# Attention row sums: one tile moved from TensorE's sums to VectorE, four sum matmuls placed behind the values, residual bias by accumulating DMAs

## The chip, the cores and the metric

The kernel runs on one core of one Trainium2 chip. A core has five engines with a queue each: TensorE (PE), VectorE (DVE), ScalarE (ACT), GpSimd (POOL) and SyncE (SP); each works through its own queue in order and waits on semaphores for the others. SP issues most DMAs; POOL issues the accumulating and the indirect ones. [...]

The metric is the device time of one execution in microseconds (us), lower is better, as the median over the runs. The profile is one more execution, taken by the hardware profiler; its own device time and its span (first to last instruction) are given beside the median below.

## The reference

A transformer block on 2 sequences of 1,024 tokens, 512 wide, in float32: attention with 16 heads of 32 and low-rank updates on all four projections, a residual and a layer norm; then a mixture of 8 experts with a capacity of 256 tokens each, a shared expert, a residual and a layer norm. Cut to what matters here:

```python
def lora_linear(x, W, b, Bm, Am):
    out = jnp.einsum('bld,od->blo', x, W) + b
    upd = jnp.einsum('blr,or->blo', jnp.einsum('bld,rd->blr', x, Bm), Am)
    return out + SCALING * upd
...
scores = jnp.einsum('bhqd,bhkd->bhqk', q, k) * SCALE
attn = jax.nn.softmax(scores, axis=-1)
out = jnp.einsum('bhqk,bhkd->bhqd', attn, v)
B, H, L, hd = out.shape
out = out.transpose(0, 2, 1, 3).reshape(B, L, H * hd)
return lora_linear(out, Wo, bo, Bo, Ao)
...
x = _layernorm(x + _L0_attn_ref(x, ...), axis=-1)
x = _layernorm(x + _L0_ffn_ref(x, ...), axis=-1)
```

## The kernel before

**Stages.** Projections of q, k and v come first (to about 157 us of the span), then the attention loop (to about 600), with the output projection of the first sequence inside it and that of the second at its end, then the router, the shared expert and the experts. The change touches the attention loop and what is fed into it.

**Units and steps.** A unit is four heads of one sequence against half of its queries (512): 16 units (`NU`). A unit has eight steps, one for each 128 keys: 128 steps `t = 8u + k` (`NS`). A step has four quarters, one per head. In a quarter PE computes the scores of 128 keys by 512 queries into PSUM (`st`, L638), and ACT takes the exponential of them into a tile `pt` in SBUF (L647); two heads share a `pt` tile of 128x1024, so a step makes two, "pair 0" and "pair 1", from a pool of 13 buffers (`PTB`). The `st` banks come from a pool of three.

**The order is written out by hand.** In this loop the instructions of all engines stand in program order (`manual_schedule`). For each quarter the loop collects a list `between[q]`, and `st_step` runs the list after that quarter's score and exponential. Into these lists go, at places given by tables at the top of the file:

- `maxima` (`S_AT`): one score tile `s` of 128 queries by 512 keys on PE (L203) and its row maximum on DVE (L211), for a unit one and a half ahead. There are 32 a unit; `s` has four PSUM banks. After a unit's last one the maxima are gathered (L214), transposed on PE (L221), split into a high and a low part (`mh` on ACT, L224; `ml` on DVE, L225), and two DMAs on SP write them as two rows into that unit's query tile (L227). The next unit's scores read these rows, so that the maximum is subtracted within the score matmul.
- `av_step` (in the fourth quarter of even steps, `AVQ`): the values, PE matmuls of 128x32 by 128x512 for the two steps before (L657), accumulated in PSUM over a unit; `av_out` copies them out on ACT in step 0 of the next unit (L671).
- `adds` (`ADDS`): the row sums of the exponentials, tile by tile. In a unit up to the 14th: step 1's tile is the base `accs`; tile 2 is added to it and tile 3 to tile 0 by accumulating DMAs that POOL issues (L682); tiles 4, 5, 6 and 0 are added on POOL (L685), for both pairs. Units 14 and 15 add on DVE instead.
- `finish` (`FIN`): the sum over partitions. Matmuls with a ones matrix (L698) turn `accs` into sums in PSUM, four matmuls, one per head; tiles named by `DIRECT` get four matmuls of their own. Then ACT copies the sums (`rc`, L712), SP writes them to DRAM (`sd`, L714) and reads them back spread over partitions (`r`, L716).
- `invert` (`REC`): the reciprocal on DVE (L722), written to DRAM (L723) and read back as rows for all partitions (`rb`, four DMAs, L726), all on SP.
- `normalize` (`NRM`): in the unit after next of its own, in three parts: DVE multiplies the values by `rb` (L738), ACT rounds the product to its high part (L743), DVE forms the low part (L745).
- `oproj` (`OPROJ_AT`): the output projection of the first sequence (L771), in units 8 to 10; DVE adds the residual row (L776) and starts the norm.
- `load_res` (`RES_AT`) reads a tile of 128 rows of the residual on SP (L750); `add_res` (`RES_ADDS`) adds the bias of the output projection to it on POOL (L754). There are 16 such tiles.

At a unit's first step SP also loads the keys (in even units, two ahead) and queries (L166, L186) of units to come. A matmul of these float32 kinds (`av`, `sm`) shows as two entries in the profile.

Which tables the change rewrites: `DIRECT`, `FIN`, `REC`, `NRM`, `S_AT`, `OPROJ_AT`, `RES_ADDS`; which lines of the loop: the place of `finish_max(NU - 1)` and of `add_res`, and a new function beside `adds`. The entry of a table under `None` holds for all units that have no entry of their own; a triple is (units later, step, quarter). A step of `S_AT` has four pairs: maxima ahead of and behind the values and the sum of that quarter.

Of the kernel before, what the change touches and what calls it, by code (L numbers as in the profile page):

```python
# [13 lines left out]
ALU = mybir.AluOpType  # L14
# [5 lines left out]
B, L, D = 2, 1024, 512  # L20
NU = 16
# [11 lines left out]
LEAD = 12  # L33
LATE, OP_ONE = (0,), 0
NS = NU * 8
# [15 lines left out]
MAN3 = {mybir.EngineType.PE}  # L51
MAN4 = MAN2 - MAN3

DIRECT = {None: (7,), NU - 2: (), NU - 1: (6, 7)}
AVQ = 3


FIN = {None: (1, 4, 1), NU - 3: (1, 3, 1), NU - 2: (1, 2, 3)}
REC = {None: (1, 6, 3), NU - 3: (1, 5, 1)}
NRM = {  # L60
    None: ((2, 3, 0), (2, 3, 0), (2, 3, 2)),
    NU - 3: ((1, 7, 3), (1, 7, 3), (1, 7, 3)),
    NU - 2: ((1, 4, 1), (1, 4, 1), (1, 4, 1)),
}


S_AT = (
    ((2, 0), (0, 0), (1, 0), (0, 0)), ((0, 0), (2, 0), (1, 0), (0, 1)),
    ((0, 0), (1, 1), (0, 1), (0, 0)), ((0, 0), (1, 1), (0, 1), (0, 1)),
    ((0, 1), (1, 1), (1, 1), (2, 0)), ((0, 0), (0, 2), (1, 0), (0, 1)),  # L70
    ((0, 1), (1, 0), (1, 0), (0, 0)), ((0, 1), (0, 1), (0, 1), (0, 1)),
)
XTB = 2


# [2 lines left out]
    NU - 2: {1: "bb1 dd01", 3: "dd23 vv4", 4: "vv5", 5: "vv6", 6: "vv3 vv7"},  # L78
    NU - 1: {1: "bb1 dd01", 3: "dd23 vv4", 4: "vv5", 6: "vv3"},
}  # L80
OPROJ_AT = (68, 70, 72, 74, 76, 78, 80, 82)
RES_AT = tuple(8 * i + (2 if i % 2 else 6) for i in range(8)) + (70, 74, 86, 90, 100, 102, 106, 110)
RES_ADDS = tuple(t + 3 for t in RES_AT[:14]) + (114, 115)
RB = 2
BTB = 4
AHEAD = 5
# [26 lines left out]
def kernel(  # L113
# [3 lines left out]
    pe, act, dve, pool, sp = nc.tensor, nc.scalar, nc.vector, nc.gpsimd, nc.sync  # L117

    def f(ap):
        return ap.bitcast(F32)  # L120
# [16 lines left out]
    bo_bc = const.tile([P, D], F32, name="bo_bc")  # L137
# [25 lines left out]
    def load_k(g, cs=slice(0, 1024), hs=slice(0, 4)):  # L163
        kt = Ks[g % 2]
        for blk, hl in ((0, 0), (1, 1), (2, 0)):
            sp.dma_start(  # L166
                out=f(kt[32 * blk : 32 * blk + 32, hs, cs]),
                in_=qk_d[1, g // NG, g % NG, hl].rearrange("(h p) t -> p h t", p=32)[:, hs, cs],
            )

    def load_v(g):
        if g < NG:
            vts[g] = x1b[:, :, g * P : g * P + P]
        else:
            vts[g] = mp_.tile([P, 8, P], F32, name=f"vt{g}", tag="vt", bufs=2)
        sp.dma_start(
            out=vts[g],
            in_=v_d[g // NG].rearrange("(c p) d -> p c d", p=P)[
                :, :, (g % NG) * P : (g % NG) * P + P
            ],  # L180
        )

    def load_q(u, hs=slice(0, 4)):
        g, qb = u // 2, u % 2
        for blk, hl in ((0, 0), (1, 0), (2, 1)):
            sp.dma_start(  # L186
                out=f(Qs[u % 3][32 * blk : 32 * blk + 32, hs]),
                in_=qk_d[0, g // NG, g % NG, hl].rearrange("(h p) t -> p h t", p=32)[
                    :, hs, qb * 512 : qb * 512 + 512
                ],  # L190
            )

    mts, pts, avs, accs, vts = {}, {}, {}, {}, {}
# [25 lines left out]
    def finish_max(u):  # L219
        mp = one.tile([P, 512], F32, name=f"mp{u}", tag="one")  # L220
        pe.transpose(mp[0:16, 0:P], mts[u], ident)  # L221
        mh = mp_.tile([16, P], F32R, name=f"mh{u}", tag="mh", bufs=2)
        ml = mp_.tile([16, P], F32R, name=f"ml{u}", tag="ml", bufs=2)
        act.copy(mh, mp[0:16, 0:P])  # L224
        dve.tensor_tensor(ml, mp[0:16, 0:P], f(mh), ALU.subtract)  # L225
        for i, m_ in enumerate((mh, ml)):
            sp.dma_start(  # L227
                out=f(Qs[u % 3][96 + i : 97 + i, :, :]).rearrange(
                    "o h (q t) -> o (h q) t", t=P
                ),  # L230
                in_=f(m_),
            )
# [236 lines left out]
    def new_xt(nm, i):  # L469
        if i % 2 == 0:  # L470
            pairs[nm] = [
                po["flx"].tile([P, KC, 512], F32R, name=f"xt{q}{nm}{i}", tag=f"xt{q}", bufs=XTB)
                for q in "hl"
# [120 lines left out]
    x1 = (x1a, x1b)  # L594
# [24 lines left out]
    with ph2, tc.manual_schedule(engines={mybir.EngineType.PE}):  # L619
# [31 lines left out]
        def av_step(t):  # L651
            u, kc = t // 8, t % 8
            g = u // 2
            if kc == 0:
                avs[u] = avp.tile([P, 512], F32, name=f"av{u}", tag="av")
            for h in range(4):
                pe.matmul(  # L657
                    avs[u][32 * h : 32 * h + 32, :],
                    vts[g][:, kc, 32 * h : 32 * h + 32],
                    pts[t, h // 2][:, h % 2, :],  # L660
                    start=kc == 0,
                    stop=kc == 7,
                    skip_group_check=True,
                )
# [4 lines left out]
        def av_out(u):  # L669
            raws[u] = ap.tile([P, 512], F32, name=f"ae{u}", tag="ae", bufs=2)  # L670
            act.copy(raws[u], avs[u])  # L671

        def adds(t):
            u, kc = t // 8, t % 8
            for op in ADDS.get(u, ADDS[None]).get(kc, "").split():
                i = u * 8 + int(op[2])
                for pr in range(2):
# [5 lines left out]
                    else:  # L683
                        eng = dve if op[pr] == "v" else pool
                        eng.tensor_tensor(accs[u, pr], accs[u, pr], pts[i, pr], ALU.add)  # L685

        def direct(u):
            return DIRECT.get(u, DIRECT[None])

# [57 lines left out]
        def load_res(n):  # L747
            b, i = divmod(n, 8)
            r0 = b * L + i * P
            sp.dma_start(out=x1[b][:, i, 0:D], in_=x[r0 : r0 + P, :])  # L750

        def add_res(n):
            b, i = divmod(n, 8)
            pool.tensor_tensor(x1[b][:, i, 0:D], x1[b][:, i, 0:D], bo_bc, ALU.add)  # L754

        later = []
        rows1 = {}
# [26 lines left out]
        def run(gen):  # L784
            for _ in gen:
                pass
# [12 lines left out]
        def at_step(table, t, q):  # L799
            for v in range(max(t // 8 - 2, 0), t // 8):  # L800
                at = table.get(v, table[None])
                at = at[q] if isinstance(at[0], tuple) else at
                if (v + at[0]) * 8 + at[1] == t:
                    yield v

        for t in range(NS):
            u, k = t // 8, t % 8
            if k == 0:

                if u % 2 == 0 and 2 <= u and u // 2 + 1 < B * NG:  # L810
                    for hs in (slice(0, 2), slice(2, 4)):
                        load_k(u // 2 + 1, hs=hs)
                        load_q(u + 2, hs)
                elif u >= 1 and u + 2 < NU:
                    load_q(u + 2)
                if u % 2 and NG <= u // 2 + 1 < B * NG:
                    load_v(u // 2 + 1)
            if t in RES_AT:
                load_res(RES_AT.index(t))
            between = [[], [], [], []]  # L820
            for q in range(4):
                between[q] += [maxima] * S_AT[k][q][0]
            if t + LEAD == NS + 1:
                between[0].append(lambda: finish_max(NU - 1))

            if t and t % 2 == 0:
                between[AVQ].append(lambda: (av_step(t - 2), av_step(t - 1)))
                if k == 0:
                    between[AVQ].append(lambda: av_out(u - 1))
            for v in at_step(FIN, t, 0):  # L830
                between[FIN.get(v, FIN[None])[2]].append(lambda v=v: finish(v))
            for q in range(4):
                between[q] += [maxima] * S_AT[k][q][1]
            if t:
                between[AVQ].append(lambda: adds(t - 1))
            for q in range(3):
                for v in at_step(NRM, t, q):
                    between[NRM.get(v, NRM[None])[q][2]].append(lambda v=v, q=q: normalize(v, (q,)))
            for v in at_step(REC, t, 0):
                if v < RDIR:  # L840
                    between[REC.get(v, REC[None])[2]].append(lambda v=v: invert(v))
            if t in RES_ADDS:
                between[3].append(lambda: add_res(RES_ADDS.index(t)))

            if t in OPROJ_AT:
                op0 = oproj(0, OPROJ_AT.index(t), OPER)
                for q in range(3):
                    between[q].append(lambda q=q, op0=op0: run(op0) if q == 2 else next(op0))
            st_step(t, between)
            for _, fn in [x for x in later if x[0] == 0]:  # L850
                fn()
            later[:] = [(n - 1, fn) for n, fn in later if n]
            if t - NS >= OPROJ1:
                next(op10, None)
# [349 lines left out]
    for st, (blk, nb) in enumerate(BLOCKS):  # L1204
        hss = []
        for c in range(6):
# [9 lines left out]
            if c == 0 and blk + nb == NB:  # L1216
                reads_xd(
                    sp.dma_start(
                        out=meta, in_=xd_d[:, D : D + 2].rearrange("(j p) c -> p j c", p=P)
# [9 lines left out]
            for v in range(c * nb, c * nb + nb):  # L1229
                bv, cv = blk + v // 6, v % 6  # L1230
                n = (bv - NB + 1) * 6 + cv
# [10 lines left out]
    with tc.manual_schedule(engines=MAN4):  # L1242
        last = None
        for e in range(E):
            nxt = e + 1
            hss = []
            for c in range(6):
# [4 lines left out]
                n = nxt * 6 + c  # L1252
# [113 lines left out]
```

## Time and profile before

| | us |
|---|---|
| median of 3 runs | 1041.44 |
| lowest and highest | 1038.62, 1042.34 |
| the profiled execution | 1041.44 |
| its span | 1039.7 |
| mean granted TensorE clock | 0.992 |

Units in the profile, from the first exponential of one to that of the next: 24.25 (unit 0), 25.46, 25.84, 26.93, 25.87, 27.13, 25.86, 26.35 (7), 31.44, 37.64, 32.10 (8 to 10, with the output projection), 27.02, 25.86, 31.76, 24.04 (14).

How to read what follows. A line of a group or of a timeline names the source line, the engine, the operation and the tiles, output before input (buffer numbers left out). In a timeline the first two columns are the start and the length in us; several like instructions in a row are merged (x8), and brackets tell how long the engine was idle before and what released it. In the list of groups the columns after the bar are the busy time in us, the mean length of one in ns, and the idle time just before them. PE's matmuls overlap, so the length of one is more than the distance to the next.

### The profile page before, as it was taken

The numbers are of one execution on the slowest core, as the hardware profiler recorded it, in microseconds if no ns is written. First come the engines' busy times: TensorE is split into PE (matmuls) and PEld (weight loads), VectorE is DVE, ScalarE is ACT, GpSimd is POOL, SyncE is SP. The second block draws the span as 40 slices with busy tenths as digits, with TensorE's granted clock in tenths as the row PEclk, the third lists the DMA queues.
The fourth block names the chain that finished last, engine by engine and source line by source line (L and its number), as shares of the span: only waits on it lengthen the run. The fifth ranks groups of instructions, "written<-read, shape, count | busy, mean of one in ns | idle before, by whom it ended". The sixth has DMA issues, their size and how long they took to land. (4 is left out here: it accounts for less than half of the span.)

```text
span 1039.7 us, 15687 instructions
## 1 busy us (share of the span) xinstructions
PE 1007.0 (97%) x5606; PEld 728.0 (70%) x5606; DVE 684.1 (66%) x1156; ACT 527.8 (51%) x1000; POOL 535.0 (51%) x404
## 2 busy tenths in 40 slices
PE   8999999999999999999989999999999999999994
PEld 6888885555545555655544489888787899999994
DVE  6743788788888887788878773232253467777752
ACT  5322216666767665576657835122122366555662
POOL 5000005989898977869887164000015055666774
PEclk9999999999999999999989999999999999999998
DMA  9866875586868784667964631000009567777621
GB/s 277 289 230 214 245 222 114 126 190 138 190 134 194 154 193 95 127 138 151 197 153 85 151 112 62 22 21 11 31 30 302 177 205 233 258 244 254 222 82 61
DMA packets 87374, 164.75 MB, mean 158 GB/s; under 512 B 15944, under 2 KB 24648, under 8 KB 87296
## 3 DMA queue, kind: packets, MB, share of 16 engines
q1 hardware_dynamic: 74240, 117.59, 38.9%
q0 software_dynamic: 13056, 46.16, 19.9%
q8 instruction: 44, 0.72, 0.3%
q14 instruction: 34, 0.28, 0.1%
HBM read 96.10 MB, written 33.80 MB: 125 GB/s over the span
## 5 line engine op out<-in xcount | busy, mean ns | idle before, releaser
L211 DVE TENSOR_REDUCE mt<-s 128x1 f32<-128x512 f32 x512 | 317.8, 680 | 69.1 <-PE s L203 68.8
L647 ACT ACTIVATE pt<-st 128x512 f32<-128x512 f32 x512 | 266.6, 611 | 113.7 <-PE st L638 107.1
L685 POOL TENSOR_TENSOR pt<-pt,pt 128x1024 f32<-128x1024 f32 x112 | 264.3, 2389 | 37.1 <-ACT pt L647 18.6
L638 PE MATMUL st<-qs,ks 98*128 98x512 f32 x512 | 197.7, 417 | 11.1 <-ACT pt L647 8.8
L203 PE MATMUL s<-ks,qs 96*128 96x512 f32 x512 | 186.8, 403 | 0.2
L638 PEld LDWEIGHTS st<-qs,ks 98*128 98x128 f32 x512 | 92.8, 189 | 94.5 <-ACT pt L647 37.9
L682 POOL DMA_DIRECT2D pt<-pt x64 | 56.2, 1004 | 185.6 <-issue 144.6
L931 PE MATMUL h<-xthe,w13s 128*128 128x256 f32 x704 | 130.0, 283 | 0.0
L203 PEld LDWEIGHTS s<-ks,qs 96*128 96x128 f32 x512 | 97.3, 190 | 36.2 <-DVE mt L211 10.8
L931 PEld LDWEIGHTS h<-xthe,w13s 128*128 128x128 f32 x704 | 110.7, 191 | 0.4
L919 POOL TENSOR_TENSOR w2s<-w2r,w2s 128x512 fp32r<-128x512 f32 x42 | 65.9, 1590 | 68.2 <-ACT w2s L918 65.3
L931 PE MATMUL h<-xtle,w13s 128*128 128x256 f32 x352 | 100.3, 285 | 0.4 <-DVE xtle L484 0.4
L1121 POOL DMA_INDIRECT xd_d<-x1a,slot_i x8 | 7.9, 984 | 139.3 <-DVE slot_i L1118 137.2
L931 PEld LDWEIGHTS h<-xtle,w13s 128*128 128x128 f32 x352 | 67.4, 191 | 1.5 <-DVE xtle L484 0.8
L657 PE MATMUL av<-pt,vt 128*32 128x512 f32 x512 | 62.3, 598 | 0.0
L657 PE MATMUL av<-pt,x1b 128*32 128x512 f32 x512 | 61.6, 598 | 0.0
L1017 PE MATMUL y<-w2s,hs 128*128 128x512 f32 x260 | 60.9, 390 | 0.0
L1017 PEld LDWEIGHTS y<-w2s,hs 128*128 128x128 f32 x260 | 48.2, 188 | 10.2 <-DVE hs L999 0.5
L342 ACT ACTIVATE oh<-o,bqk_sb 128x512 fp32r<-128x512 f32 x32 | 22.0, 690 | 56.2 <-PE o L327 52.5
L586 DVE TENSOR_TENSOR w13s<-x1a,w13s 128x1024 fp32r<-128x1024 f32 x32 | 46.7, 1460 | 4.6 <-issue 4.1
L327 PE MATMUL o<-xh,wh 128*128 128x512 f32 x116 | 45.5, 392 | 1.0 <-DVE ol L343 1.0
L327 PE MATMUL o<-xl,wh 128*128 128x512 f32 x116 | 45.3, 391 | 0.0
(571 smaller groups left out, 1704.2 us busy)
## 6 DMA issues: line engine op xcount, KB each, us to landing
pt<-pt POOLq DMA_DIRECT2D x64, 512.0 KB
x1a<-in_w_dram SPq DMA_DIRECT2D x32, 512.0 KB
w2r<-in_w_dram SPq DMA_DIRECT2D x42, 256.0 KB
ks<-qkd SPq DMA_DIRECT2D x36, 256.0 KB
qkd<-oh SPq DMA_DIRECT2D x32, 256.0 KB
qkd<-ol SPq DMA_DIRECT2D x32, 256.0 KB
qs<-qkd SPq DMA_DIRECT2D x30, 256.0 KB
qs<-qkd SPq DMA_DIRECT2D x36, 128.0 KB
```

What stands on the lines that cost most here:

```text
L203: pe.matmul(s1, Qs[u % 3][0:96, h, qt * P : qt * P + P], Ks[g % 2][0:96, h, kh * 512 : kh * 512 + 512], start=True, stop=True,)
L211: dve.tensor_reduce(mts[u][:, c, kh : kh + 1], s1, AX.X, ALU.max)
L327: pe.matmul(o, lhs, rhs, start=k + i == 0, stop=k + i == KC + 1)
L586: (pool if e < 0 else dve).tensor_tensor(lo, raw, f(hi), ALU.subtract)
L638: pe.matmul(sb, Ks[g % 2][:, h, kc * P : kc * P + P], Qs[u % 3][:, h, :], start=True, stop=True,)
L647: act.activation(pts[t, h // 2][:, h % 2, :], sb, AF.Exp, scale=SCALE)
L657: pe.matmul(avs[u][32 * h : 32 * h + 32, :], vts[g][:, kc, 32 * h : 32 * h + 32], pts[t, h // 2][:, h % 2, :], start=kc == 0, stop=kc == 7 ...
L682: pool.dma_start(out=pts[to, pr], in_=pts[i, pr], accum_op=ALU.add)
L685: eng.tensor_tensor(accs[u, pr], accs[u, pr], pts[i, pr], ALU.add)
L919: pool.tensor_tensor(hl[:, 1, :], raw, f(hl[:, 0, :]), ALU.subtract)
L931: pe.matmul(hp[:, j * 256 : j * 256 + 256], lhs, rhs[:, k, :], start=n == 0, stop=n == 11,)
L1017: pe.matmul(o, lhs, rhs, start=n == 0, stop=n == 16)
```

## The change

The last `pt` tile of a unit (step 7) was summed by PE alone (`DIRECT`, four extra matmuls a unit). It is now added to `accs` by DVE: `add_last`, in the next unit, pair 0 in step 3 behind the third head, pair 1 in step 4 behind the first head, for units 0 to 13. The sum is four matmuls, in the fourth quarter of step 4, behind that quarter's values; it stood in the second quarter. The reciprocal moves from step 6 to step 7, the three parts of the normalization by a few quarters, the maxima are spread anew over the steps, the output projection comes two steps later, the transposing of the last unit's maxima one step earlier. The bias is added to a residual tile by an accumulating DMA that POOL issues, in step 3 of each unit up to the 14th, with four in steps of their own. Units 14 and 15 keep their sums; unit 13's is no longer a case of its own.

```diff
-DIRECT = {None: (7,), NU - 2: (), NU - 1: (6, 7)}
+DIRECT = {None: (), NU - 1: (6, 7)}
 AVQ = 3
...
-FIN = {None: (1, 4, 1), NU - 3: (1, 3, 1), NU - 2: (1, 2, 3)}
-REC = {None: (1, 6, 3), NU - 3: (1, 5, 1)}
+FIN = {None: (1, 4, 3), NU - 2: (1, 2, 3)}
+REC = {None: (1, 7, 1)}
 NRM = {
-    None: ((2, 3, 0), (2, 3, 0), (2, 3, 2)),
-    NU - 3: ((1, 7, 3), (1, 7, 3), (1, 7, 3)),
+    None: ((2, 2, 3), (2, 3, 2), (2, 4, 1)),
+    NU - 3: ((2, 1, 2), (2, 1, 2), (2, 1, 2)),
     NU - 2: ((1, 4, 1), (1, 4, 1), (1, 4, 1)),
 }
...
 S_AT = (
-    ((2, 0), (0, 0), (1, 0), (0, 0)), ((0, 0), (2, 0), (1, 0), (0, 1)),
-    ((0, 0), (1, 1), (0, 1), (0, 0)), ((0, 0), (1, 1), (0, 1), (0, 1)),
-    ((0, 1), (1, 1), (1, 1), (2, 0)), ((0, 0), (0, 2), (1, 0), (0, 1)),
-    ((0, 1), (1, 0), (1, 0), (0, 0)), ((0, 1), (0, 1), (0, 1), (0, 1)),
+    ((0, 1), (0, 0), (0, 1), (1, 1)), ((1, 0), (1, 1), (1, 0), (0, 1)),
+    ((0, 0), (1, 0), (1, 0), (0, 0)), ((1, 0), (0, 1), (0, 0), (2, 0)),
+    ((0, 0), (0, 1), (0, 1), (0, 2)), ((0, 1), (0, 0), (0, 1), (2, 0)),
+    ((0, 1), (0, 1), (0, 0), (1, 1)), ((0, 0), (3, 0), (1, 0), (1, 0)),
 )
+
+
+LAST_AT = ((3, 2), (4, 0))
...
-OPROJ_AT = (68, 70, 72, 74, 76, 78, 80, 82)
+OPROJ_AT = (70, 72, 74, 76, 78, 80, 82, 84)
...
-RES_ADDS = tuple(t + 3 for t in RES_AT[:14]) + (114, 115)
+RES_ADDS = tuple(range(11, 108, 8)) + (107, 114, 115)
...
+        def add_last(u, pr):
+            dve.tensor_tensor(accs[u, pr], accs[u, pr], pts[u * 8 + 7, pr], ALU.add)
+
...
-            pool.tensor_tensor(x1[b][:, i, 0:D], x1[b][:, i, 0:D], bo_bc, ALU.add)
+            pool.dma_start(out=x1[b][:, i, 0:D], in_=bo_bc, accum_op=ALU.add)
...
-            if t + LEAD == NS + 1:
-                between[0].append(lambda: finish_max(NU - 1))
...
+            if t + LEAD == NS:
+                between[AVQ].append(lambda: finish_max(NU - 1))
...
-            if t in RES_ADDS:
-                between[3].append(lambda: add_res(RES_ADDS.index(t)))
+            for pr in range(2):
+                if 0 < u < NU - 1 and LAST_AT[pr][0] == k:
+                    between[LAST_AT[pr][1]].append(lambda pr=pr: add_last(u - 1, pr))
+            for n, at in enumerate(RES_ADDS):
+                if at == t:
+                    between[3].append(lambda n=n: add_res(n))
```

## The prediction

> **What bounds the kernel now.** I read the engine shares first, then the busy time of two neighbouring units of the attention loop, the groups of that loop, and the timelines of units 5 and 6.
>
> ```profile
> PE 1007.0 (97%) x5606; PEld 728.0 (70%) x5606; DVE 684.1 (66%) x1156; ACT 527.8 (51%) x1000; POOL 535.0 (51%) x404
> ```
>
> The windows hold one odd and one even unit:
>
> ```profile
> 285.00:311.00 26.00, 24.60 (x142) 12.65 (x141) 22.25 (x36) 17.23 (x35) 23.84 (x15) 1.00 0.64 134
> 311.00:337.00 26.00, 25.88 (x147) 13.69 (x146) 21.67 (x38) 18.27 (x38) 22.82 (x13) 1.00 0.88 189
> ```
>
> Columns after the length: PE, PEld, DVE, ACT, POOL. PE is full in the even unit; DVE (22) and POOL (23) have about 3 us to spare. Step 0 of units 5, 6 and 7 starts on ACT at 285.22, 312.35 and 338.21: the units take 27.13 and 25.86 us. The groups that the change touches:
>
> ```profile
> L698 PE MATMUL sm<-pt,ones 128*32 128x512 f32 x256 | 33.1, 626 | 0.0
> L738 DVE TENSOR_TENSOR ae<-ae,rb 128x512 f32<-128x512 f32 x14 | 22.7, 1620 | 0.5 <-DMA rb<-rd 0.4
> L685 DVE TENSOR_TENSOR pt<-pt,pt 128x1024 f32<-128x1024 f32 x16 | 18.5, 1209 | 1.7 <-DMA pt<-pt 1.7
> L754 POOL TENSOR_TENSOR x1a<-x1a,bo_bc 128x512 f32<-128x512 f32 x8 | 9.6, 1194 | 0.0
> ```
>
> L738 takes 1.62 us on average, but 0.69 where POOL is not adding. The timeline shows why odd units are longer:
>
> ```profile
> 292.15 2.38 POOL L685 TENSOR_TENSOR pt<-pt,pt 128x1024 f32<-128x1024 f32 x1
> 293.50 2.83 DVE L738 TENSOR_TENSOR ae<-ae,rb 128x512 f32<-128x512 f32 x1
> ...
> 294.48 1.30 POOL L754 TENSOR_TENSOR x1a<-x1a,bo_bc 128x512 f32<-128x512 f32 x1
> ...
> 296.36 0.62 ACT L743 CAST at_h<-ae 128x512 fp32r<-128x512 f32 x1 [1.17 <-DVE ae L738]
> ...
> 297.53 0.50 PE L638 MATMUL st<-qs,ks 98*128 98x512 f32 x1 [1.40 <-ACT pt L647]
> ```
>
> L738 reads two SBUF tiles and ends 0.55 after POOL's second addition (295.78): it was held through both. ACT waits for it, and PE for ACT. Unit 13 does this with two L754 (L738: 4.33 us), and PE's idle time brings the clock down:
>
> ```profile
> 532.99 0.80 PE L638 MATMUL st<-qs,ks 98*128 98x512 f32 x1 [2.63 <-ACT pt L647]
> ...
> 535.00 3.62 PE L698 MATMUL sm<-pt,ones 128*32 128x512 f32 x16
> ```
>
> Sixteen entries take 3.62 us there, not 1.92; the granted clock is 0.5 from 531.64 for 6.83 us.
>
> A second path is nearly as long as PE's. SP's queue in unit 6:
>
> ```profile
> 327.13 0.54 SPq L714 DMA_DIRECT2D sd<-rc  x1
> 332.91 0.33 SPq L716 DMA_DIRECT2D r<-sd  x1
> 333.33 0.52 SPq L227 DMA_DIRECT2D qs<-mh  x1
> 333.94 0.54 SPq L227 DMA_DIRECT2D qs<-ml  x1
> ```
>
> ```profile
> 337.72 0.40 PE L638 MATMUL st<-qs,ks 98*128 98x512 f32 x1
> ```
>
> L716 waits 5.6 us for the sums to land in DRAM, and the maxima's rows (L227), which unit 7's first score reads at 337.72, stand behind it in the queue. By the semaphore updates they land at 336.94, 0.78 us ahead. Over the units without output projection the time from L714 to that landing is 8.3 to 10.4 us, and the margin 0.2 to 2.3.
>
> **The change part by part.** Positions are us from a unit's first score matmul; rows are unit 5's and 6's.
>
> *Sums.* 14 units lose four of eight matmuls (8 of 16 entries). The block takes 1.85 us (324.53 to 326.38) plus 0.2 for switching in and out (0.32 and 0.34 between starts, against 0.234). Eight entries behind the values take 0.85 and switch nothing: 1.2 us less PE time, 14 x 1.2 = 16.7. PE's floor for a plain unit: 64 matmuls x 0.234 + 4 value blocks x 2.05 + 0.85 + transposing 0.27 = 24.3; the same sum gives 25.5 for before (measured 25.86).
>
> *Bias.* 16 POOL additions (19.7 us) become 16 accumulating DMAs. Issuing one took POOL 0.88 us (56.2/64), 14 us in all, in the pause after its last addition. Their data (4 MB) follow the unit's own DMAs on the queue; the first reader is a projection three steps or more later, against a 4 to 7 us landing for twice the size. I cost it at nothing; without that cover it is late by at most one landing, 5 us, once. Without L754, L738 (now a quarter step earlier) waits for one addition at most. Gone are PE waits of 0.60, 1.40, 0.59, 1.25 and 2.63 (at 244, 297, 349, 477, 532), 6.5 us, and half of the 5.5 us at half clock, 2.7: together 9.2.
>
> *DVE.* 28 additions at 1.21 (start to start 1.14, the L685 rows) are 2.3 us a unit, against 0.9 less for L738: DVE goes from 22 to 23.5 of at least 24.3, so it is no bound. Behind them in its queue stand reductions; PE may be four PSUM tiles (2.4 us) ahead before it waits. What the additions wait for, POOL's last one, is done by 9.3 (below); what waits for them is ACT, which now takes the buffers they free at 12.5 and 16.9, and they end at 12.4 and 14.7. ACT's buffers of steps 6 and 7 now wait for the last two accumulating DMAs, which land 9.2 to 14.6 after the first issue (295.72 to 304.92; 215.97 to 230.49), so at 19 to 24.6, and are wanted at 19.7 and 22.5: nothing in odd units, up to 2 in even ones, inside PE's wait at the unit's end (next part); without that wait 2 x 6 = 12.
>
> *Return path.* The sums now end after step 4's values, at 15.5 instead of 14.5; rc and L714 follow 0.75 later, at 16.3. SP's order (L714, L716, L227) is unchanged. Adding 9.4 (the middle of 8.3 to 10.4) and 0.14 (unit 15: 573.78 to 573.92), the next unit's first score can't start before 25.8. PE would be done at 24.3 and waits 1.5. L722 stands at 25 and its operand lands some 0.4 before the maxima's rows (336.57, 336.94), so it may hold DVE 0.5; L738's rows land some 6 after it, 2 ahead of need. So in ten plain units (1 to 7, 11 to 13) the 1.2 us are not gained: 12 of 16.7 are lost. At 8.3 the unit takes 24.7, at 10.4 it takes 26.8: 10 us either way over ten units. Units 8 and 9 had 6.8 us of margin; these, 10 and 14 keep their gain.
>
> *Shared read path.* L738, the additions and L745 (now behind the second one) need POOL not to add. With 0.61 per reduction DVE reaches L738 at 8.7, the additions at 11.3 and 13.6, L745 at 15.5. With units of 25.8 POOL's last addition ends at 7.9 to 9.3 and the next chain starts when the first accumulating DMA lands: its issue waits for step 2's values (9.9 in unit 6, 10.0 now), plus 4.6 in odd units, 6.1 in even ones:
>
> ```profile
> 295.72 1.74 POOL L682 DMA_DIRECT2D pt<-pt  x2
> ...
> 300.33 2.39 POOL L685 TENSOR_TENSOR pt<-pt,pt 128x1024 f32<-128x1024 f32 x1 [0.72 <-DMA pt<-pt]
> 302.92 2.38 POOL L685 TENSOR_TENSOR pt<-pt,pt 128x1024 f32<-128x1024 f32 x1 [0.20 <-DMA pt<-pt]
> ```
>
> So POOL starts at 14.7 (odd) and 16.1 (even). The additions come in time; L745 does by 0.6 in even units, and in the six odd ones (3 to 13) it is 0.8 late. If it gets in at the 0.2 us gap after POOL's first addition it waits 1.6 and PE some 1.5, of which 1.0 lies in the wait at the unit's end: 0.6 x 6 = 3.6. The other end is a rival below; the low end is nothing.
>
> [...]
>
> The order and places of the other steps (maxima, projections two steps later, unit 13's late sum) I take as nothing: DVE's last chain has 1.74 + 0.84 + 0.68 us of idle time before L708 and L685 to take it up; uncovered, 0 to 3 us.
>
> Sum: 1041.44 (the profiled execution, which is also the median; span 1039.7 and 1.7 around it) - 16.7 + 12 - 9.2 + 3.6 = **1031**.
>
> **The rivals.** *The whole gain*: the maxima's rows land early and no collision. 1041.4 - 16.7 - 9.2 = 1015.5. For it: PE at 25.88 of 26; against: margins of 0.2 to 2.3 us that the change cuts by 2.5.
>
> *Return path at its long end* (10.4, as in units 2 and 12): nothing is won but the 9.2 and 4.7, 10 are lost: 1037.5; and waits of 2.5 may halve the clock (1.40 did not, 2.63 did), 2.7 each: two of them give 1043, no change. [...]
>
> *Slower: POOL keeps the read path.* If POOL goes from addition to addition without letting L745 in, as from L685 to L754 at 294.48, DVE stands until POOL lacks input. The gap that would let it in is 0.2 us, and the new DMA issue may close it. Let in after two additions, L745 is 4 us late, PE idles 2.8 more and loses 2.7 to the clock: 5.5 x 6 = 33, so 1041.4 - 13.9 + 33 = 1060; after three it is 9 x 6 = 54, 1081. It decides from a delay of about 3 us in the odd units. Against it: VectorE did get in between two L919 at 873.
>
> **How the numbers follow.** Forecast 0.40 (own range 1022 to 1037), whole gain 0.12, long return path 0.16, slower 0.32. The range takes 1017 to 1062: below lies part of the whole gain, above the worse half of the slower case. Half a per cent is 5.2 us, about what a measurement can tell: below 1036.2 lie the forecast but 0.03, the whole gain and 0.01 of the third, 0.50; within it 0.13; above 1046.6 the rest, 0.37.
>
> **What would show it.** Sums of 8 entries right behind values; PE idle ahead of the first score of each plain unit, released by qs<-ml; no L754; L738 at 0.7 to 1.2; additions at 1.2; L745 at 0.7 in even and 2.2 in odd units. Wrong if the first scores don't wait (whole gain), or if L745 takes 4 us and the clock falls in many units (slower).

## The result, and the profile after

The changed kernel takes 1055.3 us (median of 6 runs, 1047.7 to 1060.1), beside 1040.7 us before (6 runs, 1036.4 to 1042.3). The ratio is 1.0146, with a 95% interval of 1.0120 to 1.0172: about 15 us slower, where 10 us faster was forecast; it lies in the upper part of the range given. The profiled execution took 1056.53 us with a span of 1054.5.

First the engine line of the page of the changed kernel, then the groups that the change touches, from the groups of 160 to 640 us (columns: line, engine, operation, tiles, count | busy us, mean ns of one | idle us just before them, and what ended it):

```profile
PE 1011.3 (96%) x5494; PEld 729.7 (69%) x5494; DVE 717.6 (68%) x1184; ACT 531.3 (50%) x1000; POOL 532.1 (50%) x404
```

```profile
L641 PE MATMUL st<-qs,ks 98*128 98x512 f32 x506 | 199.1, 428 | 28.0 <-DVE ml L228 13.1 <-ACT pt L650 12.8 <-DMA qs<-ml 1.9
...
L691 DVE TENSOR_TENSOR pt<-pt,pt 128x1024 f32<-128x1024 f32 x28 | 34.0, 1214 | 0.0
...
L751 DVE TENSOR_TENSOR at_l<-ae,at_h 128x512 fp32r<-128x512 f32 x15 | 23.2, 1550 | 0.1
...
L704 PE MATMUL sm<-pt,ones 128*32 128x512 f32 x144 | 19.3, 593 | 0.0
...
L744 DVE TENSOR_TENSOR ae<-ae,rb 128x512 f32<-128x512 f32 x14 | 10.5, 753 | 0.4 <-DMA rb<-rd 0.3
```

Line numbers are 3 to 10 higher than before: L641 is the score matmul (L638), L744 the first normalising step (L738), L751 the low part (L745), L228 the low part of the maxima (L225). What the change was to do, it did: the sums are down from 256 entries to 144, L744 takes 0.75 us instead of 1.62, the new additions (L691) take 1.21 and are never held. But L751 now takes 1.55 on average instead of 0.68, and the score matmuls wait 13.1 us for L228 and 12.8 for ACT.

The loop grew by 21.4 us between the start of unit 1 and that of unit 15 (393.3 to 414.7). What came ahead of it was 2.1 shorter, and the stretch after it 4.6 (465.3 to 460.7). Seven kernels of the experiments, with nearly the same code there, also lie at 460.3 to 462.3 in that stretch and the others at up to 464.9; no cause was found. Within the loop:

| us, units 1 to 14 | before | after |
|---|---|---|
| PE idle, sum of its waits | 9.4 | 27.2 |
| time at half clock | 6.8 (1 stretch) | 34.1 (7 stretches) |
| loop less the waits and half of the half-clock time outside them | 381.2 | 372.4 |

So there was a saving of some 9 us (an estimate that takes a half-clock stretch to cost half its length, as the sixteen entries of the prediction's row did, 3.62 us instead of 1.92 at a granted clock of 0.50), and it was lost three times over, in two ways that take turns: odd units wait for L228, even units for ACT.

**Odd units.** Timeline of unit 3, which starts at 233.16 (columns: start, length, engine, line; in brackets the idle time and its releaser):

```profile
246.72 1.21 DVE L691 TENSOR_TENSOR pt<-pt,pt 128x1024 f32<-128x1024 f32 x1
...
247.48 2.68 POOL L688 TENSOR_TENSOR pt<-pt,pt 128x1024 f32<-128x1024 f32 x1
...
248.66 2.04 DVE L751 TENSOR_TENSOR at_l<-ae,at_h 128x512 fp32r<-128x512 f32 x1
...
250.50 4.74 POOL L688 TENSOR_TENSOR pt<-pt,pt 128x1024 f32<-128x1024 f32 x2 [0.34 <-DMA pt<-pt]
250.63 1.28 DVE L214 TENSOR_REDUCE mt<-s 128x1 f32<-128x512 f32 x2
251.83 0.27 DVE L228 TENSOR_TENSOR ml<-mp,mh 16x128 fp32r<-16x128 f32 x1
...
252.16 0.50 PE L641 MATMUL st<-qs,ks 98*128 98x512 f32 x1 [1.51 <-DVE ml L228]
```

POOL's chain begins 14.3 us into the unit, L751 is reached at 15.5 and let in at POOL's pause after its first addition. L228 stands two reductions behind it and is the last reader of the PSUM buffer that the next score matmul writes: it comes at 18.7 instead of the even units' 17.2, and PE stands for about as long as L751 was held (1.4 us). Units 5, 7 and 11 are the same (L751 2.05, 2.62, 2.34; PE 1.36, 1.92, 1.65). Unit 9 is the exception: its L751 starts just ahead of POOL's chain and is not held. Unit 13 is worse. The table RES_ADDS puts one bias DMA into step 3 of each of the units 1 to 13 and a second one into that of unit 13; the last two stay in unit 14:

```profile
548.66 2.08 POOL L760 DMA_DIRECT2D x1b<-bo_bc  x2
...
549.89 7.83 POOL L688 TENSOR_TENSOR pt<-pt,pt 128x1024 f32<-128x1024 f32 x3
...
550.92 7.36 DVE L751 TENSOR_TENSOR at_l<-ae,at_h 128x512 fp32r<-128x512 f32 x1
...
559.72 0.80 PE L641 MATMUL st<-qs,ks 98*128 98x512 f32 x1 [6.66 <-DVE ml L228]
```

Here POOL's three additions follow each other with no pause, and L751 is held through all of them.

**Even units.** Timeline of unit 4, which starts at 261.47, POOL, SP and the waits of ACT and PE only:

```profile
263.28 1.99 SPq L732 DMA_DIRECT2D rb<-rd  x4
...
265.37 1.31 SPq L169 DMA_DIRECT2D ks<-qkd  x3
...
270.05 2.99 SPq L189 DMA_DIRECT2D qs<-qkd  x3
...
271.24 2.65 POOL L685 DMA_DIRECT2D pt<-pt  x3 [4.28 <-PE st L641]
...
280.98 2.35 POOL L688 TENSOR_TENSOR pt<-pt,pt 128x1024 f32<-128x1024 f32 x1 [5.13 <-DMA pt<-pt]
...
283.49 1.08 ACT L650 ACTIVATE pt<-st 128x512 f32<-128x512 f32 x2 [1.47 <-DMA pt<-pt]
...
284.14 0.79 PE L641 MATMUL st<-qs,ks 98*128 98x512 f32 x1 [1.56 <-ACT pt L650]
```

The unit's key and query loads (L169, L189) begin 3.9 us into the unit, behind the broadcast of the reciprocals (L732). Before, they began at 0.7 (unit 4 of the kernel before starts at 259.35):

```profile
260.03 1.31 SPq L166 DMA_DIRECT2D ks<-qkd  x3
```

The accumulating DMAs issued at 271.24 move their first packet at 275.42, 4.2 us later (2.3 in unit 4 before, 1.4 in odd units), when 2.24 of the 2.62 MB of the broadcast and the loads have moved. So POOL's chain starts at 19.5 (16.2 in unit 4 before), the buffers of the last steps come free late, ACT waits for them (pt<-pt) and PE for ACT: 1.7 to 2.5 us in units 2, 4, 6 and 12.

**The clock.** Stretches of 3.41 us of the changed kernel (columns: busy us and count of PE, PEld, DVE, ACT, POOL, then the granted clock, DMA share, GB/s):

```profile
249.38:252.79 3.41, 1.90 (x9) 1.23 (x8) 3.41 (x6) 1.75 (x5) 3.07 (x2) 1.00 1.05 207
252.79:256.20 3.41, 3.41 (x10) 2.63 (x9) 3.25 (x6) 2.33 (x4) 3.41 (x3) 0.50 0.95 182
307.40:310.81 3.41, 2.60 (x18) 1.03 (x10) 3.38 (x5) 1.85 (x4) 2.70 (x2) 1.00 1.06 205
310.81:314.22 3.41, 2.86 (x12) 2.11 (x12) 3.41 (x7) 2.25 (x5) 3.41 (x2) 1.00 1.06 207
314.22:317.63 3.41, 3.41 (x23) 1.61 (x23) 2.73 (x6) 1.54 (x4) 3.41 (x3) 1.00 0.34 61
```

Every change of the clock in the loop falls on one grid of 3.41 us: the seven stretches at half begin 0, 9, 26, 34, 71, 81 and 89 steps of it after 252.79. Unit 3's wait lies inside one of its stretches, PE is busy for 1.90 of 3.41, and the next stretch runs at half. Unit 5's wait of nearly the same length is cut in two by the grid (busy 2.60 and 2.86), and the clock stays.

### The profile page after: what moved, and what is told of

It is laid out like the page before. It is cut to its first block, busy times and chain, and to the rows that moved or that the text cites. A ratio compares the mean times of both kernels' runs of the same rounds, so it can differ in the third digit from the quotient of the medians.

```text
span 1054.5 us, 15573 instructions
## 1 busy us (share of the span) xinstructions
PE 1011.3 (96%) x5494; PEld 729.7 (69%) x5494; DVE 717.6 (68%) x1184; ACT 531.3 (50%) x1000; POOL 532.1 (50%) x404
## 5 line engine op out<-in xcount | busy, mean ns | idle before, releaser
L214 DVE TENSOR_REDUCE mt<-s 128x1 f32<-128x512 f32 x512 | 321.4, 679 | 60.2 <-PE s L206 59.6
L650 ACT ACTIVATE pt<-st 128x512 f32<-128x512 f32 x512 | 269.4, 609 | 125.2 <-PE st L641 82.7
L641 PE MATMUL st<-qs,ks 98*128 98x512 f32 x512 | 201.5, 428 | 29.1 <-DVE ml L228 13.1
L206 PE MATMUL s<-ks,qs 96*128 96x512 f32 x512 | 197.5, 420 | 1.1 <-ACT pt L650 1.0
L641 PEld LDWEIGHTS st<-qs,ks 98*128 98x128 f32 x512 | 98.8, 194 | 100.9 <-ACT pt L650 59.1
L206 PEld LDWEIGHTS s<-ks,qs 96*128 96x128 f32 x512 | 100.0, 195 | 59.8 <-issue 19.5
L660 PE MATMUL av<-pt,x1b 128*32 128x512 f32 x512 | 64.5, 623 | 0.0
L583 ACT CAST w13s<-x1a 128x1024 fp32r<-128x1024 f32 x32 | 33.4, 1045 | 24.8 <-DMA x1a<-in_w_dram 18.6
```

The lines of the kernel that those rows point to most:

```text
L206: pe.matmul(s1, Qs[u % 3][0:96, h, qt * P : qt * P + P], Ks[g % 2][0:96, h, kh * 512 : kh * 512 + 512], start=True, stop=True,)
L214: dve.tensor_reduce(mts[u][:, c, kh : kh + 1], s1, AX.X, ALU.max)
L641: pe.matmul(sb, Ks[g % 2][:, h, kc * P : kc * P + P], Qs[u % 3][:, h, :], start=True, stop=True,)
L650: act.activation(pts[t, h // 2][:, h % 2, :], sb, AF.Exp, scale=SCALE)
L660: pe.matmul(avs[u][32 * h : 32 * h + 32, :], vts[g][:, kc, 32 * h : 32 * h + 32], pts[t, h // 2][:, h % 2, :], start=kc == 0, stop=kc == 7 ...
```

## The experiments

Each was timed beside the kernel before on its own chip. The kernel before took 1039.0 to 1043.5 us there, so kernels are compared by their ratios. Unless said otherwise the diff is against the changed kernel.

| kernel | median us | ratio to before (95%) |
|---|---|---|
| changed kernel | 1055.3 | 1.0146 (1.0120 to 1.0172) |
| bias_alone | 1035.9 | 0.9977 (0.9952 to 1.0001) |
| pool_bias | 1084.6 | 1.0439 (1.0397 to 1.0482) |
| low_late | 1061.1 | 1.0169 (1.0100 to 1.0238) |
| loads_first | 1044.6 | 1.0056 (1.0023 to 1.0088) |
| low_early | 1048.0 | 1.0062 (1.0028 to 1.0095) |
| bias_rows | 1038.6 | 0.9964 (0.9940 to 0.9987) |
| loads_low | 1036.0 | 0.9930 (0.9905 to 0.9956) |
| all_three | 1033.0 | 0.9892 (0.9857 to 0.9926) |
| no_adds | 1034.1 | 0.9938 (0.9915 to 0.9961) |
| rec_back | 1057.7 | 1.0152 (1.0110 to 1.0194) |
| no_bias | 1052.1 | 1.0103 (1.0071 to 1.0134) |

Theory A: L751, held by POOL, delays L228 and so PE in odd units. Theory B: the loads' later issue delays POOL's accumulating DMAs and so ACT's buffers in even units. Rivals: the bias DMAs, VectorE simply full, the return path of the sums.

### bias_alone: only the bias DMAs, in the kernel before

```diff
-RES_ADDS = tuple(t + 3 for t in RES_AT[:14]) + (114, 115)
+RES_ADDS = tuple(range(11, 108, 8)) + (107, 114, 115)
-            pool.tensor_tensor(x1[b][:, i, 0:D], x1[b][:, i, 0:D], bo_bc, ALU.add)
+            pool.dma_start(out=x1[b][:, i, 0:D], in_=bo_bc, accum_op=ALU.add)
```

> The kernel before with its 16 POOL additions of the bias replaced by accumulating DMAs, nothing else. Theory of the prediction: L738 falls from 1.62 to at most 1.2 us, the five waits of PE (6.5 us) and the one half clock (2.7) go: 9 us less, about 1032. Rival 1 (the bias rows' 256 KB share the engines with the units' own accumulating DMAs, which land later, so ACT waits for its buffers): 1041 or more, and waits of ACT on pt<-pt appear in even units. Rival 2 (the DMA issues hold what the additions held): L738 stays above 1.5 and nothing changes, 1041.

The mechanism came as the theory had it: L738 takes 0.82 us, the waits of PE behind it are gone (what is left of its waits for ACT is 0.1 to 0.4 a unit, and 0.6 in unit 14), and there is no half clock in the loop. The time fell by 0.2% only, with an interval that touches no change; a new wait took the place of much of it:

```profile
331.81 0.33 SPq L716 DMA_DIRECT2D r<-sd  x1
...
332.23 0.52 SPq L227 DMA_DIRECT2D qs<-mh  x1
...
332.84 0.54 SPq L227 DMA_DIRECT2D qs<-ml  x1
...
338.35 0.47 PE L638 MATMUL st<-qs,ks 98*128 98x512 f32 x1 [1.18 <-DMA qs<-ml]
```

This is unit 6: the first score of unit 7 waits for the maxima's rows, which stand behind L716 in SP's queue. Such waits add up to 5.8 us, in units 2, 6, 12, 13 and 14. The margin of 0.2 to 2.3 us was a real one, and the time that L754 had cost had covered it. In the profiled loop the waits for ACT and the half clock fell by some 8 us, the waits on the rows grew by 5.0, and PE's time outside waits and half clock grew by 2 (381.2 to 383.4), for which no cause was found.

### pool_bias: the bias added by POOL again, at the new places

```diff
-            pool.dma_start(out=x1[b][:, i, 0:D], in_=bo_bc, accum_op=ALU.add)
+            pool.tensor_tensor(x1[b][:, i, 0:D], x1[b][:, i, 0:D], bo_bc, ALU.add)
```

> The changed kernel with the bias added by POOL at the same places, nothing else. If the bias DMAs are innocent, the even units' late buffers and the odd units' late low part stay, and the addition at the end of step 3 holds VectorE's second addition by up to 1.2 us: 1055 to 1068. If the bias DMAs are what makes the accumulating DMAs late in even units, the first packet comes 2 to 3 us after the issue there instead of 4.2 to 5.9, ACT's waits for pt go, and the time is 1040 to 1048.

1084.6, above the first range and far from the second. From its groups of 160 to 640 us:

```profile
L691 DVE TENSOR_TENSOR pt<-pt,pt 128x1024 f32<-128x1024 f32 x28 | 63.3, 2261 | 0.0
...
L704 PE MATMUL sm<-pt,ones 128*32 128x512 f32 x144 | 30.9, 641 | 12.1 <-DVE pt L691 12.1
```

The addition of the bias lies just ahead of VectorE's second addition, and in units 1, 3 and 5 that one takes 4.6 to 4.7 us (8.0 in unit 13) instead of 1.2, through the bias and POOL's first addition, with the sums behind it. At these places the DMAs are worth some 30 us; at the places of the kernel before, with the rest of the change, POOL additions were not tried.

### low_late: the low part behind the maxima's

```diff
-    None: ((2, 2, 3), (2, 3, 2), (2, 4, 1)),
+    None: ((2, 2, 3), (2, 3, 2), (2, 4, 3)),
```

> The changed kernel with the low part (L751) behind the maxima's low part (L228) on VectorE, half a step later. Theory A (L751, held by POOL in odd units, makes L228 late, PE waits for the PSUM buffer that L228 reads, and its clock halves): the waits of PE on L228 (13 us) and five of the seven half clocks (27 us at half, so 13) go, less some wait for reductions behind L751: 1030 to 1040. Rival (the hold only moves on to the reductions, four PSUM tiles are no cover): PE waits on L214 instead, 1050 to 1056.

The rival had the mechanism right, and the time, 1061.1, is above its range. L228 comes on time, and the reductions behind L751 are late instead (groups of 160 to 640 us):

```profile
L206 PE MATMUL s<-ks,qs 96*128 96x512 f32 x458 | 180.7, 424 | 19.5 <-DVE mt L214 18.0 <-ACT pt L650 1.0
...
L751 DVE TENSOR_TENSOR at_l<-ae,at_h 128x512 fp32r<-128x512 f32 x15 | 26.3, 1756 | 0.1
```

The four PSUM tiles of scores are no cover: PE stood 1.8 to 3.0 us in units 2, 3, 5, 6 and 11 and 6.6 in unit 13. So it is the hold that costs, whatever stands behind it.

### low_early: the low part ahead of POOL's chain

```diff
-    None: ((2, 2, 3), (2, 3, 2), (2, 4, 1)),
+    None: ((2, 2, 3), (2, 3, 2), (2, 3, 3)),
-LAST_AT = ((3, 2), (4, 0))
+LAST_AT = ((3, 1), (3, 3))
```

> The changed kernel with L751 ahead of VectorE's second addition (end of step 3) and the additions a quarter step earlier. Theory A (every us that POOL holds L751 makes L228, and so PE, a us late, and 1.3 us of idle time in one 3.41 us window of the clock's halves it): L751 takes 0.7 us in all units, PE's waits on L228 in odd units (6.4 us in units 3, 5, 7, 11 and more in 13) and their half clocks (20.5 us at half) are gone, the even units' waits for pt stay: 1055 - 15 to 20, so 1035 to 1040. Rival (VectorE is simply full there, and L228 is late without the hold): 1050 to 1056. Rival (the second addition is now the one held): L691 over 2 us in odd units, 1050 to 1060.

L751 takes 0.69 us on average, in odd units too, and L691 is not held. Unit 3 of this kernel, in the timeline:

```profile
246.62 0.68 DVE L751 TENSOR_TENSOR at_l<-ae,at_h 128x512 fp32r<-128x512 f32 x1
...
247.22 1.21 DVE L691 TENSOR_TENSOR pt<-pt,pt 128x1024 f32<-128x1024 f32 x1
...
247.34 5.68 POOL L688 TENSOR_TENSOR pt<-pt,pt 128x1024 f32<-128x1024 f32 x2
```

The waits of PE on L228 are gone in every unit, units 3, 5, 7 and 13 last 25.8 to 26.9 us instead of 26.7 to 33.7, no odd unit has a half clock, and units 2, 4 and 6 still wait 1.5 to 1.9 us for ACT. The ratio fell by 0.8% (1.0146 to 1.0062), with intervals that do not touch. That is theory A. The time is above the 1035 to 1040 expected: in the profile the loop is 16.6 us shorter (398.1), but units 11 to 13 now wait 1.2 to 1.3 us each for the maxima's rows, PE's time outside waits and half clock is 5 us longer, and the stretch after the loop is 4.2 longer, the last two without a cause found.

### loads_first: half of the loads ahead of the broadcast

SP issues rd, six loads, the broadcast, six loads, instead of rd, the broadcast, twelve loads.

```diff
+        def spread(u):
+            rd = fin[u]
+            rc = ap.tile([P, 512], F32, name=f"rb{u}", tag="rc", bufs=1)
...
                         load_k(u // 2 + 1, hs=hs)
                         load_q(u + 2, hs)
+                        if hs.start == 0:
+                            spread(u - 2)
```

> The changed kernel with the first six of an even unit's twelve key and query loads ahead of the broadcast of the reciprocals in SP's queue, which otherwise waits for L728. Theory B (L728's new place holds the loads 3 us longer, and POOL's accumulating DMAs stand behind the loads' data): the first packet in even units comes 1 to 2.5 us after the issue instead of 4.2, the waits of ACT for pt and the half clocks of even units (13.7 us at half) go: 1040 to 1047. Rival (the engines are full with 5 MB in each even unit whatever the order, or the bias rows do it): first packet still 4 us late, 1052 to 1056. If the broadcast is late behind the loads, L744 starts later than 7.2 us into even units and this eats the gain.

Theory B, in the timeline of this kernel's unit 4 (start 261.0):

```profile
261.85 1.33 SPq L169 DMA_DIRECT2D ks<-qkd  x3
263.22 1.66 SPq L189 DMA_DIRECT2D qs<-qkd  x3
264.98 1.76 SPq L736 DMA_DIRECT2D rb<-rd  x4
267.38 1.38 SPq L169 DMA_DIRECT2D ks<-qkd  x3
```

The loads begin at 0.8, the first accumulating packet moves 2.8 to 3.8 us after its issue in units 2, 4 and 6 (4.2 to 5.4 in the changed kernel) and 4.5 in unit 12 (5.9), POOL's chain starts at 15.9 to 17.7 instead of 18.9 to 19.5, ACT's part of PE's waits falls from 1.7 to 2.5 us a unit to 0.5 to 0.6 (1.7 in unit 12), and the even units' half clocks are gone. The four that are left are all in odd units, with L751 as before. The ratio is 1.0056.

### rec_back: the reciprocal back at its old place

```diff
-REC = {None: (1, 7, 1)}
+REC = {None: (1, 6, 3)}
```

> The changed kernel with L728 (the reciprocal of the sums) back at the end of step 6, where it was before. Theory B (L728's place in VectorE's queue is what holds the loads): the even units' loads are issued about 2 us earlier, the first packet comes 2 to 3.5 us after POOL's issue, ACT's waits for pt and the even units' half clocks shrink: 1044 to 1050, the odd units as before. Rival (the sums land too late for that place, VectorE stands waiting for them and the reductions behind it are late): PE waits on L214, 1053 to 1062, and the loads are no earlier than in loads_first.

Both happened, and cancelled (1057.7). The loads begin at 1.7 to 1.9 in even units and PE's waits for ACT fall to about 1 us (1.7 in unit 12), but L728 stands waiting for sums that land too late for it, and PE waits for a reduction behind it for 1.0 to 1.2 us in units 2, 4, 6 and 12. So L728's place is not the root: it follows from the sums, which end at 16.1 instead of 14.1 us into an even unit.

### bias_rows and loads_low: the return path and both theories together

bias_rows is bias_alone with the sums' load (the DRAM read that waits for sd) issued three quarters of a step later, behind the maxima's rows:

```diff
-            sp.dma_start(out=r16, in_=sd.rearrange("h (j c) -> (h j) c", c=16))
+            for v in at_step(FIN, t - 1, 0) if t else ():
+                if v < RDIR:
+                    between[0].append(lambda v=v: fetch(v))
```

> The kernel before with the bias DMAs (as in bias_alone, 1035.9) and the maxima's rows ahead of the sums' load in SP's queue. Return path theory: the waits of PE on the rows (5.8 us in units 2, 6, 12, 13, 14 of bias_alone) go and nothing else changes: 1029 to 1032. Rival (the rows land late because the DMA engines are busy with the residual and accumulating DMAs, not because of the queue): waits of 0.7 to 1.2 stay, 1035 to 1037.

The waits on the rows are gone in units 2, 6, 12 and 13; unit 14's 2.3 stays. But units 3, 5, 7 and 13 now wait 0.6 to 1.1 us for reductions, one with a half clock behind it, and the ratio (0.9964) can't be told from bias_alone's. The queue was the cause of the waits; removing them brought the next one.

loads_low is loads_first and low_early together:

> The changed kernel with loads_first's order and low_early's places together. Theories A and B together: half clocks gone but for one at most, L751 at 0.7; then the return path ends plain units at 25.8, as the prediction had it, with PE waits on the maxima's rows: 1022 to 1030. If the return path is no bound (the prediction's term of 12 us was wrong for good), plain units take 25.0 to 25.3: 1014 to 1021. If A or B falls: above 1035.

1036.0, ratio 0.9930, on a chip where the kernel before took 1043.5. That is past the 1035 at which A or B was to have fallen, but the trace shows both at work: there is no half clock in the loop, L755 (the low part) takes 0.69 us. Plain odd units take 25.8 us, even ones 26.6 to 27.2, with 0.4 to 1.3 us of waits on the rows in units 2 and 11 to 13. So the range was too low: neither of its ends had ACT's waits in the even units, of which 0.5 to 0.9 us are left. It also took the odd units' 25.8 for the return path's doing; units 3, 5 and 7 reach it without any wait on the rows.

### all_three: with the maxima's rows first as well

> loads_low and the maxima's rows ahead of the sums' load. Return path theory: the waits on the rows go, plain units take 25.0 to 25.3 and the time is 6 to 10 us under loads_low's. Rival (something else, VectorE or ACT's buffers, already ends the units): within 3 us of loads_low.

1033.0, ratio 0.9892, the lowest of all, 1.1% below the kernel before. The waits on the rows are gone but for unit 14's. Odd units take 25.6 to 26.0, but even ones stay at 26.9 to 27.9. PE's waits for ACT, 0.6 to 1.2 us in these, are part of that, and the rest has no cause shown. The gain on loads_low is 3 us, with overlapping intervals, so the rival holds about as well.

### no_adds: all_three without the additions

The diff is against all_three.

```diff
-DIRECT = {None: (), NU - 1: (6, 7)}
+DIRECT = {None: (7,), NU - 2: (), NU - 1: (6, 7)}
-FIN = {None: (1, 4, 3), NU - 2: (1, 2, 3)}
+FIN = {None: (1, 4, 1), NU - 2: (1, 2, 3)}
-LAST_AT = ((3, 1), (3, 3))
+LAST_AT = ()
```

> all_three without VectorE's additions: the last tile goes back into the sums (16 entries at the place of the kernel before, a half step earlier); what is left of the change is the bias DMAs and the places. By the prediction's term the additions save 1.2 us in 14 units: 1.6% over all_three, ratio to before 1.005. By the rows of the traces (the block of sums 1.85 us before, 1.28 after): 0.6 x 14 = 8 us over all_three, ratio 0.997. Rival (the additions save nothing, since VectorE and ACT's later buffers take it back): ratio 0.985 to 0.991.

0.9938 beside 0.9892: the additions are worth some 5 us in the best surroundings found, but the intervals overlap, so this is not clear of noise. In the profiled executions the loop is 391.0 and 388.6 us: PE has 6.5 us less to do with the additions (loop less waits and half clock, 383.7 and 377.2) and gives 4 back in waits.

### no_bias: without the bias DMAs

This kernel leaves out adding the bias to the 14 blocks of units 1 to 13.

```diff
-                if at == t:
+                if at == t and n > 13:
```

> The changed kernel without the bias in 14 of the 16 residual row blocks (units 1 to 13): their accumulating DMAs are left out, all else stays. The prediction costed them at nothing. If so: 1052 to 1058, same waits. Rival (256 KB more on full engines delays the rows, loads and buffers of each unit): the even units' waits of ACT for pt and their half clocks shrink, 1042 to 1050. Whatever the unit, unit 13, which has two of them, must keep its 6.7 us wait on L228 if the bias DMAs are not what holds L751 there.

1.0103, some 4 us below the changed kernel, with intervals that touch. The even units' waits for ACT stay (1.9 to 2.7 us in units 2, 4, 6 and 12), and those of units 3 and 5 on L228 (1.3); units 7 and 11 have none, in unit 7 because POOL's chain starts at 15.9, behind L751. But unit 13 is not as expected: L751 takes 2.26 us instead of 7.36 and PE waits 1.57 instead of 6.66. With two bias DMAs issued just ahead of it, POOL's first addition takes 3.2 us instead of 2.4, its next input is there before it ends, and POOL's record shows no pause that would let L751 in. That this is why is argued, not shown: loads_first has the same two DMAs in unit 13, its record shows no pause either, and the low part gets in after POOL's first addition (2.79 us). The kernel is not a clean one for the DMAs' cost: in units 9 and 10 POOL's addition now comes first and holds L751 (2.91 us each), and PE waits 1.4 to 1.5 us there that the changed kernel does not have.

## Why the prediction was wrong

*Shared read path: right in place and length, wrong in price. This is the step that failed.* Forecast: L751 (then L745) on time in even units, late in odd ones, let in after POOL's first addition, held some 1.6 us. It was so in units 3, 5, 7 and 11 (held 1.4 to 1.9). The step went on: PE waits "some 1.5, of which 1.0 lies in the wait at the unit's end: 0.6 x 6 = 3.6". None of it lay in such a wait. PE stood for all of it, 6.4 us in units 3, 5, 7 and 11 and 6.7 in unit 13, and the clock halved in four of these five units for 20.5 us, which cost some 9 more (3.3 of the 20.5 lie within the waits). So the term of 3.6 became some 22 in the profile. The forecast for these units was 25.8 + 0.6 = 26.4 us. Unit 5, with the wait alone, takes 26.7; units 3, 7 and 11, with a half clock, 28.3 to 30.3; unit 13, held through three additions, 33.7. So the step left out the clock, which it took to need a wait near 2.5, and a hold beyond one addition. That one addition would end the hold was the author's estimate, and no run shows what ends it. Nor does a run show a path that VectorE and POOL share; what the traces show is L751 at 0.68 us where none of POOL's additions was running when it came, and at 2.04 to 7.36 in these five units, where one was. low_early, which takes the hold away, is 0.8% faster, some 9 us, and its profiled loop 16.6 us shorter.

*Return path, 12 us: it was there, but not as forecast.* The wait at the end of each plain unit was both charged and used as cover for two other costs. In the changed kernel PE waits on the rows for 0.4 to 0.7 us in four units only, because the units are 26.7 to 33.7 us long and the rows land in time: the cover was gone as soon as the first wait replaced it. It was also thinner than forecast: less waits and half clock, units 1, 3, 5, 7 and 11 take 24.8 to 25.2 us of PE's time, not 24.3, which leaves at most 1.0 of the 1.5 below 25.8. Where the other waits are taken away, the rows do bind (5.8 us in bias_alone, 1.2 to 1.3 a unit in low_early's last units).

*Buffers of steps 6 and 7: named, and hidden behind the same wait.* "Up to 2 in even ones, inside PE's wait at the unit's end; without that wait 2 x 6 = 12." PE waited 1.7 to 2.5 us for ACT in units 2, 4, 6 and 12, and three of these had a half clock. The term was nothing in the sum; in the profile it is 8.4 us of waits and some 6.5 of half clock. What was overlooked is why it is up to 2.5: the change moves the sums 2 us later in even units, so the reciprocal, so the broadcast, and the twelve loads behind it in SP's queue. Those DMAs I did not move along. loads_first shows it: 0.9%, again some 9 us. Together with low_early (loads_low) it is 2.2%, all of the loss and more.

*Sums, 16.7: too large.* The block takes 0.97 us after (8 entries, up to the next matmul) and 1.85 before, 0.88 a unit instead of 1.2; that makes 12. The maxima's matmuls take some of it back (in unit 5, 8.56 us for 32, against 8.12 in unit 4 before). What the loop shows is some 9, and no_adds puts the additions at 5, not clear of noise.

*Bias, 9.2 gained and no cost: the waits went as said,* and bias_alone has no half clock, but only some 2 us of it reached the time: the rows' wait took 5, and PE's other time grew by 2. The cost was perhaps not quite nothing: without the DMAs unit 13's hold falls from 7.4 to 2.3 us.

*DVE 23.5 of 24.3, no bound: wrong by position.* No additions were held, but there was no room for 1.4 us of hold behind them, and low_late shows that PE's lead of four tiles covers none of it.

*The rivals.* The slower one named the right mechanism, place and units, but wanted L751 to wait through two additions and 4 us to decide. It needed 1.4. Its own trigger, three additions without a pause, came in unit 13 alone. What nearly doubled the short hold's price was the clock: the prediction took waits of 1.40 as harmless from one case and charged the clock from 2.5 on.

## What to carry to other kernels

A wait that is forecast at one place is cover for another only as far as the estimate of the work before it holds: here PE's own work was 0.5 to 0.9 us longer than estimated, and that much of the 1.5 of cover was not there. When a result moves later, follow it through the queue of the engine that sends it, with every transfer issued behind it, and ask what those transfers then collide with. Where PE is nearly full, price a recurring wait of 1.4 us or more at nearly twice its length: here a half clock of 3.41 or 6.83 us added 1.7 or 3.4 (half its length, an estimate) to some of the waits and nothing to others, some 9 us on 13.

## What the runs showed of the hardware

**The clock changed on a grid of 3.41 us.** In each of the traces with more than one half-clock stretch in the loop, all begin at whole multiples of 3.41 us from each other and last 3.41, 6.83, 10.24 or 13.65 us. In the loops of the ten traces that show a half clock, 31 stretches at full clock had 1.46 us or more of PE idle time (waits over 0.1 us added up), and the next was at half in every case; with 1.21 to 1.43 us it was in 13 of 20, with 0.94 to 1.16 in one of 20, with less in none. In the changed kernel's own trace it was seven with 1.47 to 3.41 us, all followed by a half, and none with 1.03 or less. So the wait of 1.36 us in unit 5, cut by the grid, cost no more than itself, and those of 1.51 in unit 3 and 1.65 in unit 11 some 1.7 and 3.4 us more (half of 3.41 and 6.83, an estimate). Why some half-clock stretches last longer than one step of the grid, no run here shows. A stretch idle for 1.46 of its 3.41 us, 43%, sufficed every time.

**VectorE's operation waited through one or several of POOL's additions.** L751 took 0.68 us where none was running when it came, and 2.04 (unit 3), 2.34 (unit 11) and 7.36 (unit 13) in the changed kernel. It got in at pauses of 0.34 us (unit 3, 250.16 to 250.50) and 0.1 (unit 11). Where each addition's record starts 0.5 us before the last one's ends, it waited through three (unit 13, 7.36 us). Where the records overlap by 0.1 us or less, an operation waited through two in the kernel before (the prediction's row at 293.50) and got in in unit 13 of loads_first. What decides there, no run shows.

**A transfer issued by POOL started late behind SP's loads.** In unit 4 its first packet came 4.2 us after the issue; until then 0.95 MB of SP's transfers moved and, but for one packet of instructions, nothing else. From 275.4 to 281.0 it and the rest of the loads moved side by side (0.91 and 0.38 MB). What held the first packet, no run here shows.
